# Row maxima of two neighbouring heads, scored in two row strips of the array

## The chip, the cores and the metric

The kernel runs on one core of one Trainium2 chip. The metric is device time in microseconds (us) of one execution. The engines are named as in the profile: PE is TensorE's matmuls, PEld its weight loads, DVE is VectorE, ACT is ScalarE, POOL is GpSimd, SP is SyncE, which only issues DMAs here.

## The reference

A decoder of four layers runs over `x` of 8 batches x 256 positions x 128 channels. Each layer adds three residual blocks: self-attention, cross-attention to a context of 512 positions, and a feed-forward block. Four of the attention blocks share one code path and are what the change touches. They have 16 heads of 8 channels:

```python
# layers 0 and 2, cross-attention (layer 0 with a mask), 512 keys; layer 3, self- and cross-attention, causal, 256 keys
scores = einsum('bqhd,bkhd->bhqk', qh, kh) / sqrt(8)      # (8, 16, 256, 512) or (8, 16, 256, 256)
attn = softmax(scores, axis=-1)                           # masked first, where there is a mask
ctx = einsum('bhqk,bkhd->bqhd', attn, vh).reshape(8, 256, 128)
x = x + ctx @ Wo.T + bo                                   # layer 3's second also gates the context
```

## The kernel before

**Heads in the partitions.** A head has only 8 channels. Queries and keys are split into a rounded part and a remainder, and four products of parts stand for one product of full precision, so a head takes 8 x 4 = 32 rows. `mh_k` holds two neighbouring heads for each of 8 pairs: the even head in rows 0 to 31, the odd one in rows 32 to 63, zeros in rows 64 to 95. `mh_q` holds each head by itself in its own 32 of the first 64 rows; all other rows are zero, so a matmul over 96 rows (`TOP`) gives one head's scores. Rows 96 and 97 of `mh_q` take the negated row maximum, in two parts, with ones against it in `mh_k`.

**Two passes over the scores.** Pass one (`maxima`, line 510) makes the scores with queries in the partitions, so that VectorE can reduce along a row: `mh_sps` in PSUM, reduced into `mh_nm`. With 512 keys there are two matmuls of 96 rows x 512 columns a head, one for each half of the queries, each in a bank of its own, and each reduced by VectorE: `lowest` (line 520) where there is a mask, `tensor_reduce` (line 542) where there is none. In the causal stages one bank holds both halves, 128 and 256 columns wide. `turn` (line 544, GpSimd) splits the maxima of four heads, `turned` (line 554) transposes them on TensorE (`mh_mps`) and sends them by a DMA into `mh_q`. Pass two (`exps`, line 565) makes the scores again with keys in the partitions, `mh_bsps`, with the maximum subtracted by the two extra rows, and ScalarE takes the exponent into `mh_e`. `combine` (line 614) multiplies with the values for four heads at once, each into its own 32 columns of the array (`mh_ops`, 128*32). `divide`, `finish`, `project_out` and `normed` end a batch element.

**Order.** One loop over t = 16 b + h runs over the 128 heads of 8 batch elements. Step t does `maxima(t)`, after every fourth head `turn`; then a stretch of another layer's work, the guest (layer 0's own attention, `la_` tiles, in the first stage; other blocks, `fa_` and `qf_` tiles among them, in layer 2's and the first causal stage); then `turned` for the group before, at t % 4 == 1; `exps(t - lag)`, with a lag of 8 steps or of 12 in the causal stages; `combine` every fourth step; then what was put off. Matmuls and transposes keep the order in which they are written (`mm`, line 459, records them all, so they all have line 460; transposes have line 463).

**PSUM.** Eight banks: `ps_a` has three, used in turn by `mh_sps` and `mh_ops`; `ps_b` three for `mh_bsps`; `g` two for all else.

Of the kernel before, what the change touches and what calls it, by code (L numbers as in the profile page):

```python
# [30 lines left out]
F32 = mybir.dt.float32  # L31
BF16 = mybir.dt.bfloat16
# [4 lines left out]
ALU = mybir.AluOpType  # L37
AX = mybir.AxisListType
PSUM = bass.MemoryType.PSUM

P = 128
B, S, SK, D = 8, 256, 512, 128
# [4 lines left out]
TOP = 96  # L47
FLOOR = -1.0e20
# [296 lines left out]
class _Heads:  # L345
# [113 lines left out]
    def mm(self, *a, **kw):  # L459
        return self.E.tc.keep_in_program_order(self.E.nc.tensor.matmul(*a, **kw))  # L460
# [17 lines left out]
def _heads_attention(E, ctx, causal=False, mask=None, key_bias=None, gate=False, guest=None, known=(0,), pace=None):  # L478
# [6 lines left out]
    hd, nc, W = E.heads, E.nc, E.w(E.heads.layer)  # L485
    n, ready = hd.n, hd.ready
# [5 lines left out]
    wk = pool("mh", 2)  # L492
# [3 lines left out]
    ps_a = ctx.enter_context(E.tc.tile_pool(name="mh_pa", bufs=3, space=PSUM))  # L496
    ps_b = ctx.enter_context(E.tc.tile_pool(name="mh_pb", bufs=3, space=PSUM))
    mm = hd.mm
# [8 lines left out]

    units, extras = {}, {}

    def maxima(t):  # L510

        b, h = divmod(t, H)
        if h == 0 and key_bias:
            extras[b] = key_bias(b)
        if h % 4 == 0:
            u = units[t // 4] = SimpleNamespace(r=ready[b], es={}, extra=extras.get(b))
            u.nm = sm.tile([P, 2, 4], F32, name="mh_nm")
        u = units[t // 4]
        q, k = u.r.q[:TOP, h, :], u.r.k[:TOP, h // 2, :]
        def lowest(at, scores, lowered):  # L520

            rest = wk.tile([P, S if causal else n], BF16, name="mh_rest")
            nc.vector.tensor_tensor_reduce(  # L523
                rest[:, : scores.shape[1]], scores, lowered, -1.0, -FLOOR, ALU.add, ALU.min, accum_out=at
            )

        col = slice(h % 4, h % 4 + 1)
        if causal:
            ps = ps_a.tile([P, 3 * P], F32, tag="a", name="mh_sps")
            mm(ps[:, :P], q[:, :P], k[:, :P], start=True, stop=True, skip_group_check=True)  # L530
            mm(ps[:, P:], q[:, P:], k, start=True, stop=True, skip_group_check=True)
            by = (u.extra or E.causal)[0].rearrange("p i k -> p (i k)")
            lowest(u.nm[:, 0, col], ps[:, :P], by[:, :P])
            lowest(u.nm[:, 1, col], ps[:, P:], by[:, P:])
            return
        for c in range(2):
            ps = ps_a.tile([P, n], F32, tag="a", name="mh_sps")
            mm(ps, q[:, c * P : c * P + P], k, start=True, stop=True, skip_group_check=True)
            if mask is not None:
                lowest(u.nm[:, c, col], ps, mask[0][:, c, :])  # L540
            else:
                nc.vector.tensor_reduce(u.nm[:, c, col], ps, AX.X, ALU.max, negate=True)  # L542

    def turn(i):

        u = units[i]
        nm = u.nm
        hi = sm.tile([P, 2, 4], F32R, name="mh_hi")
        nc.gpsimd.tensor_copy(hi, nm)  # L549
        u.nx = sm.tile([P, 2, 2, 4], F32, name="mh_nx")  # L550
        nc.gpsimd.tensor_copy(u.nx[:, :, 0, :], hi)
        nc.gpsimd.tensor_tensor(u.nx[:, :, 1, :], nm, hi, ALU.subtract)  # L552

    def turned(i):

        u = units[i]
        ps = pg.tile([P, 2, P], F32, tag="g", name="mh_mps")
        for c in range(2):
            turn_over(ps[:8, c, :], u.nx[:, c, :, :].rearrange("p a h -> p (a h)"))
        m = wk.tile([8, S], F32R, name="mh_m")  # L560
        nc.scalar.copy(m, ps[:8].rearrange("p c q -> p (c q)"))  # L561
        h0 = 4 * (i % 4)
        nc.scalar.dma_start(u.r.q[TOP : TOP + 2, h0 : h0 + 4, :].bitcast(F32), m.bitcast(F32))

    def exps(t):

        u, h = units[t // 4], t % H
        if causal:
            ps = ps_b.tile([P, 384], F32, tag="b", name="mh_bsps")
            if u.extra:  # L570
                mm(ps, E.ident16, u.extra[1], start=True, stop=False, skip_group_check=True)
            else:
                mm(
                    ps.rearrange("p (i q) -> p i q", q=P)[:, 0:3:2, :], E.later,
                    E.ident16.unsqueeze(1).to_broadcast([P, 2, P]), start=True, stop=False, skip_group_check=True,
                )
            for kt in range(2):
                mm(
                    ps[:, 256 * kt : 256 + P * kt], u.r.k[:, h // 2, kt * P : kt * P + P],
                    u.r.q[:, h, kt * P :], start=False, stop=kt == 1, skip_group_check=True,  # L580
                )
            e = pe.tile([P, 384], F32, tag="e", name="mh_e")
            nc.scalar.activation(e, ps, AF.Exp, scale=scale)  # L583
            u.es[h % 4, 0], u.es[h % 4, 1] = e[:, :S], e[:, S:]
            return
        for kt in range(0, nk, 2):
            ps = ps_b.tile([P, 2, S], F32, tag="b", name="mh_bsps")
            if mask is not None:
                mm(ps, E.ident16, mask[1][:, kt : kt + 2, :], start=True, stop=False, skip_group_check=True)
            for j in range(2):  # L590
                mm(
                    ps[:, j, :], u.r.k[:, h // 2, (kt + j) * P : (kt + j + 1) * P], u.r.q[:, h, :],
                    start=mask is None, stop=True, skip_group_check=True,
                )
            e = pe.tile([P, 2, S], F32, tag="e", name="mh_e")
            nc.scalar.activation(e, ps, AF.Exp, scale=scale)  # L596
            u.es[h % 4, kt], u.es[h % 4, kt + 1] = e[:, 0, :], e[:, 1, :]
# [5 lines left out]
    def gate_of(b):  # L603
        ps = pg.tile([P, 2, D], F32, tag="g", name="mh_gps")
        for c in range(2):
            mm(ps[:, c, :], E.xt(b)[:, c * P : c * P + P], W("wg"), start=True, stop=True)
        gates[b] = gp.tile([P, 2, D], F32, name="mh_gates")
        nc.vector.tensor_tensor(gates[b], ps, W("bg").unsqueeze(1).to_broadcast([P, 2, D]), ALU.add)

        nc.scalar.activation(gates[b], gates[b], AF.Exp, scale=-1.0)  # L610
        nc.vector.tensor_scalar(gates[b], gates[b], 1.0, None, ALU.add)
        nc.vector.reciprocal(gates[b], gates[b])  # L612
# [68 lines left out]
    def visit(rate):  # L681

        credit[0] += rate
        while credit[0] >= 1:
            credit[0] -= 1
            normed_already.add(next(guest, None))
# [3 lines left out]
    t, end = 0, H * B + lag + 4  # L690
    while t < end or todo:
        now[0] = t
        b, h = divmod(t, H)
        if b + 1 < B:
            if h == 0:
                early, spread, values = hd.steps(b + 1)
            if causal:

                at = {2: early[:1], 3: early[1:2], 4: early[2:], 13: [values]}
                at.update({5 + i: spread[i : i + 1] for i in range(6)})  # L700
            else:
                at = {6: early[:1], 8: spread[:1], 9: spread[1:2] + early[1:], 13: spread[5:] + [values]}
                at.update({10 + i: spread[2 + i : 3 + i] for i in range(3)})
            while h == (2 if causal else 9) and b + 1 not in normed_already:
                visit(1)
            for f in at.get(h, ()):
                f()
        if gate and b < B and h == 6:
            gate_of(b)
        if t < H * B:  # L710
            maxima(t)
            if t % 4 == 3:
                turn(t // 4)
        if guest:
            visit(pace(t))
        if t % 4 == 1 and 4 < t < H * B + 2:
            turned(t // 4 - 1)
        if 0 <= t - lag < H * B:
            exps(t - lag)
        c = t - lag - 4  # L720
        if c % 4 == 0 and 0 <= c < H * B:
            combine(c // 4)
        for f in todo.pop(t, ()):
            f()
        if t == H * (B - 2) + 12 + free:
            E.draining()
        if t in E.amid:
            E.amid.pop(t)()
        t += 1
# [4 lines left out]
def _l0(E, names, given_up):  # L734

    nc = E.nc
    with ExitStack() as scope, ExitStack() as first:
# [39 lines left out]
        for _ in queries:  # L777
            pass
        _heads_attention(E, scope, mask=(m, mt), guest=steps, pace=lambda t: 2.4 if t < 9 else 1.4)


def _l2_xattn(E, ctx):
    guest, E.guest = E.guest, None
    _heads_attention(E, ctx, guest=guest, known=(0, 1), pace=lambda t: 1.25)


def _l3_attn(E, ctx):
    guest, E.guest = E.guest, None
    _heads_attention(E, ctx, causal=True, guest=guest, known=(0, 1), pace=lambda t: 0.6)
# [992 lines left out]
```

## Time and profile before

| | |
|---|---|
| median of two runs | 1774.6 us (1774.25 and 1774.94) |
| span of the profiled execution, first to last instruction | 1770.2 us |
| PE busy | 1462.7 us, 83% |
| PEld busy | 1055.3 us, 60% |
| DVE busy | 1148.5 us, 65% |
| ACT busy | 881.5 us, 50% |
| POOL busy | 495.7 us, 28% |
| mean granted TensorE clock | 0.928 |
| `mh_sps` matmuls, 96x512 | 512, mean 457 ns |
| `mh_sps` matmuls, 96x256 and 96x128 | 256 each, mean 355 and 322 ns |
| reduction of 128x512 scores on DVE | 685 ns with the mask, 680 without |

The profile is of one execution. A matmul's row lasts from its start to its modelled end, and rows overlap, so what a matmul costs TensorE is read from one start to the next. "128x512" is partitions x elements; "96*128" are the rows and columns of the array that an instruction uses. "[0.19 <-PE mh_sps L460]" at a row's end says that the engine stood idle for 0.19 us before it and what it waited for. A line of waits gives the total in us, the number of times, and the longest. A line of a window gives its start and end, its length, then for each engine busy time and the number of instructions, and then the granted clock, the share of the DMA engines and GB/s.

The four stages of the change lie at 62 to 495 us (layer 0), 894 to 1265 (layer 2), 1339 to 1510 and 1528 to 1690 (layer 3).

### The profile page before, as it was taken

Reading aid. Unit: us, or ns where it says so; the run is one execution under the profiler, and the core shown is the slowest. Engines: PE = TensorE matmul, PEld = TensorE weight load, DVE = VectorE, ACT = ScalarE, POOL = GpSimd, SP = SyncE. Lnnn points to the kernel's source line nnn. Section 1 sums busy time; section 2 is a strip of 40 time slices with the busy share of each in tenths; the row PEclk is TensorE's granted clock in tenths of the full one; section 3 lists DMA queues with packets and bytes.
Section 4 is the critical chain, followed back from the end, with each engine's and each line's share of the span. In section 5 each row is a group of like instructions: output and inputs, shape, how many; then the busy total and the mean of one; then the engine's idle time right before and its main releaser. Section 6 shows DMA issues by size and latency. Waiting matters only on the chain. (4 is left out here: it accounts for less than half of the span.)

```text
span 1770.2 us, 29308 instructions
## 1 busy us (share of the span) xinstructions
PE 1462.7 (83%) x10103; PEld 1055.3 (60%) x10141; DVE 1148.5 (65%) x3857; ACT 881.5 (50%) x1830; POOL 495.7 (28%) x987
## 2 busy tenths in 40 slices
PE   5689989999999998785578888878946799799986
PEld 3457677766665555453446666656615677677763
DVE  4567666765636676777667777767465666466756
ACT  7245455555652344325535655557644466355543
POOL 3122222221110122223433433332113433244422
PEclk9799999999999999997979999989956899899998
DMA  4011011104100000000111101111002221122100
GB/s 154 13 37 36 6 34 37 36 11 155 38 1 1 1 1 1 0 1 1 36 35 36 28 14 37 37 37 45 2 10 65 85 69 38 50 55 59 39 1 25
DMA packets 47236, 60.43 MB, mean 34 GB/s; under 512 B 5232, under 2 KB 36976, under 8 KB 46448
## 3 DMA queue, kind: packets, MB, share of 16 engines
q1 hardware_dynamic: 44720, 56.99, 11.9%
q8 instruction: 80, 1.31, 0.3%
q10 hardware_dynamic: 2368, 1.57, 0.3%
q14 instruction: 68, 0.56, 0.1%
HBM read 14.50 MB, written 1.05 MB: 9 GB/s over the span
## 5 line engine op out<-in xcount | busy, mean ns | idle before, releaser
L460 PE MATMUL mh_sps<-mh_k,mh_q 96*128 96x512 f32 (+2 forms) x1024 | 323.4, 398 | 49.0 <-DMA mh_q<-mh_qp 16.9
L460 PE MATMUL mh_bsps<-mh_q,mh_k 128*128 128x256 f32 (+1 forms) x1536 | 352.7, 335 | 7.6 <-ACT mh_e L596 4.1
L596 ACT ACTIVATE mh_e<-mh_bsps 128x512 f32<-128x512 f32 x512 | 281.0, 599 | 117.6 <-PE mh_bsps L460 110.4
L460 PEld LDWEIGHTS mh_bsps<-mh_q,mh_k 128*128 128x128 f32 x1536 | 265.8, 198 | 32.6 <-issue 6.9
L460 PEld LDWEIGHTS mh_sps<-mh_k,mh_q 96*128 96x128 f32 x1024 | 172.5, 202 | 96.2 <-issue 35.9
L523 DVE CUSTOM_DVE_ANT_0 mh_rest<-mh_sps,mask_b 128x512 bf16<-128x512 f32 x256 | 167.2, 685 | 81.4 <-PE mh_sps L460 78.4
L460 PE MATMUL mh_ops<-mh_e,mh_v 128*32 128x256 f32 (+1 forms) x3072 | 194.0, 373 | 1.3 <-DVE mh_nm L523 0.8
L542 DVE TENSOR_REDUCE mh_nm<-mh_sps 128x1 f32<-128x512 f32 x256 | 165.0, 680 | 25.7 <-PE mh_sps L460 25.2
L583 ACT ACTIVATE mh_e<-mh_bsps 128x384 f32<-128x384 f32 x256 | 118.6, 494 | 57.8 <-PE mh_bsps L460 33.5
L460 PEld LDWEIGHTS mh_ops<-mh_e,mh_v 128*32 128x32 f32 x3072 | 94.5, 111 | 66.1 <-ACT mh_e L583 5.8
L197 POOL TENSOR_SCALAR ln_rstd<-ln_mv 128x2 f32<-128x2 f32 x96 | 22.0, 229 | 386.4 <-DVE ln_mv L195 386.1
L549 POOL CAST mh_hi<-mh_nm 128x8 fp32r<-128x8 f32 x128 | 25.0, 195 | 337.9 <-DVE mh_nm L523 211.4
L523 DVE CUSTOM_DVE_ANT_0 mh_rest<-mh_sps,causal 128x128 bf16<-128x128 f32 (+1 forms) x256 | 79.4, 352 | 51.0 <-PE mh_sps L460 49.0
L523 DVE CUSTOM_DVE_ANT_0 mh_rest<-mh_sps,km_q 128x128 bf16<-128x128 f32 (+1 forms) x256 | 79.4, 350 | 43.8 <-PE mh_sps L460 42.5
L561 ACT CAST mh_m<-mh_mps 8x256 fp32r<-8x256 f32 x128 | 46.2, 361 | 102.1 <-PE mh_mps L463 100.2
L215 ACT COPY xt<-ln_ps 128x256 f32<-128x256 f32 x96 | 36.0, 375 | 120.5 <-PE ln_ps L463 62.3
L629 ACT COPY mh_osb<-mh_ops 128x256 f32<-128x256 f32 x128 | 47.7, 372 | 83.5 <-PE mh_ops L460 83.3
L886 ACT ACTIVATE moe_si<-moe_gps 128x512 f32<-128x512 f32 x64 | 38.0, 597 | 102.5 <-PE moe_gps L884 87.6
L460 PE MATMUL mh_bsps<-mask_t,ident 128*128 128x512 bf16 x219 | 84.7, 387 | 0.4 <-ACT mh_e L596 0.4
L201 DVE TENSOR_SCALAR ln_z<-x,ln_mv,ln_rstd 128x128 f32<-128x128 f32 x136 | 43.4, 360 | 54.9 <-POOL ln_rstd L198 54.7
L884 PE MATMUL moe_ups<-xt,w_L_ffn 128*128 128x512 f32 x128 | 69.2, 623 | 6.9 <-ACT moe_si L886 4.8
L463 PE MATMUL mh_mps<-ident,mh_nx 128*8 128x128 f32 x256 | 51.1, 282 | 27.7 <-POOL mh_nx L552 23.2
(360 smaller groups left out, 3086.8 us busy)
## 6 DMA issues: line engine op xcount, KB each, us to landing
mh_k<-mh_kp SPq DMA_DIRECT2D x64, 256.0 KB
mh_q<-mh_qp SPq DMA_DIRECT2D x256, 64.0 KB
mh_k<-mh_kp SPq DMA_DIRECT2D x64, 128.0 KB
w_L_ffn<-in_w_L_ffn SPq DMA_DIRECT2D x2, 1558.0 KB
w_L_attn<-in_w_L_attn SPq DMA_DIRECT2D x2, 1056.0 KB
ctx_t<-in_ctx_t SPq DMA_DIRECT2D x4, 512.0 KB
mh_q<-mh_m ACTq DMA_DIRECT2D x128, 8.0 KB
w_L_ffn<-in_w_L_ffn SPq DMA_DIRECT2D x2, 687.0 KB
```

Of the source, the lines that this page charges most:

```text
L201: (engine or nc.vector).tensor_scalar(z[:, q, :], E.x[:, 2 * b + q, :], mv[:, q, 0:1], rstd[:, q : q + 1], ALU.subtract, ALU.mult)
L215: E.nc.scalar.copy(E.xt(b), ps.rearrange("p q t -> p (q t)"))
L460: return self.E.tc.keep_in_program_order(self.E.nc.tensor.matmul(*a, **kw))
L463: return self.E.tc.keep_in_program_order(self.E.nc.tensor.transpose(*a))
L523: nc.vector.tensor_tensor_reduce(rest[:, : scores.shape[1]], scores, lowered, -1.0, -FLOOR, ALU.add, ALU.min, accum_out=at)
L542: nc.vector.tensor_reduce(u.nm[:, c, col], ps, AX.X, ALU.max, negate=True)
L561: nc.scalar.copy(m, ps[:8].rearrange("p c q -> p (c q)"))
L583: nc.scalar.activation(e, ps, AF.Exp, scale=scale)
L596: nc.scalar.activation(e, ps, AF.Exp, scale=scale)
L629: nc.scalar.copy(osbs[b][:, u4 % 2, :], ops)
L884: nc.tensor.matmul(ps, W("w13")[:, o : o + P], xt, start=True, stop=True)
L886: nc.scalar.activation(si, pgate, AF.Silu)
```

## The change

`maxima` is called at even steps only and does two heads, t and t + 1. Each head's matmul takes only the head's own 32 rows, 0 to 31 or 32 to 63, of `mh_q` and `mh_k`, so that the two heads stand in two row strips of the array. The two heads' matmuls of one query half stand next to each other in the order and write two banks of `ps_a`. With 512 keys the two first halves are made and their reductions issued, then the two second halves; in the causal stages all four matmuls come first and then the four reductions. `lowest` moves out of `maxima` as it is. `turn` and all else stay where they were.

```diff
--- before.py
+++ after.py
@@ -507,6 +507,13 @@
 
     units, extras = {}, {}
 
+    def lowest(at, scores, lowered):
+
+        rest = wk.tile([P, S if causal else n], BF16, name="mh_rest")
+        nc.vector.tensor_tensor_reduce(
+            rest[:, : scores.shape[1]], scores, lowered, -1.0, -FLOOR, ALU.add, ALU.min, accum_out=at
+        )
+
     def maxima(t):
 
         b, h = divmod(t, H)
@@ -516,30 +523,32 @@
             u = units[t // 4] = SimpleNamespace(r=ready[b], es={}, extra=extras.get(b))
             u.nm = sm.tile([P, 2, 4], F32, name="mh_nm")
         u = units[t // 4]
-        q, k = u.r.q[:TOP, h, :], u.r.k[:TOP, h // 2, :]
-        def lowest(at, scores, lowered):
-
-            rest = wk.tile([P, S if causal else n], BF16, name="mh_rest")
-            nc.vector.tensor_tensor_reduce(
-                rest[:, : scores.shape[1]], scores, lowered, -1.0, -FLOOR, ALU.add, ALU.min, accum_out=at
-            )
-
-        col = slice(h % 4, h % 4 + 1)
+        two = range(2)
+        rows = [slice(32 * r, 32 * r + 32) for r in two]
+        q = [u.r.q[rows[r], h + r, :] for r in two]
+        k = [u.r.k[rows[r], h // 2, :] for r in two]
+        col = [slice((h + r) % 4, (h + r) % 4 + 1) for r in two]
+        go = dict(start=True, stop=True, skip_group_check=True)
         if causal:
-            ps = ps_a.tile([P, 3 * P], F32, tag="a", name="mh_sps")
-            mm(ps[:, :P], q[:, :P], k[:, :P], start=True, stop=True, skip_group_check=True)
-            mm(ps[:, P:], q[:, P:], k, start=True, stop=True, skip_group_check=True)
+            ps = [ps_a.tile([P, 3 * P], F32, tag="a", name="mh_sps") for r in two]
+            for r in two:
+                mm(ps[r][:, :P], q[r][:, :P], k[r][:, :P], **go)
+            for r in two:
+                mm(ps[r][:, P:], q[r][:, P:], k[r], **go)
             by = (u.extra or E.causal)[0].rearrange("p i k -> p (i k)")
-            lowest(u.nm[:, 0, col], ps[:, :P], by[:, :P])
-            lowest(u.nm[:, 1, col], ps[:, P:], by[:, P:])
+            for r in two:
+                lowest(u.nm[:, 0, col[r]], ps[r][:, :P], by[:, :P])
+                lowest(u.nm[:, 1, col[r]], ps[r][:, P:], by[:, P:])
             return
         for c in range(2):
-            ps = ps_a.tile([P, n], F32, tag="a", name="mh_sps")
-            mm(ps, q[:, c * P : c * P + P], k, start=True, stop=True, skip_group_check=True)
-            if mask is not None:
-                lowest(u.nm[:, c, col], ps, mask[0][:, c, :])
-            else:
-                nc.vector.tensor_reduce(u.nm[:, c, col], ps, AX.X, ALU.max, negate=True)
+            ps = [ps_a.tile([P, n], F32, tag="a", name="mh_sps") for r in two]
+            for r in two:
+                mm(ps[r], q[r][:, c * P : c * P + P], k[r], **go)
+            for r in two:
+                if mask is not None:
+                    lowest(u.nm[:, c, col[r]], ps[r], mask[0][:, c, :])
+                else:
+                    nc.vector.tensor_reduce(u.nm[:, c, col[r]], ps[r], AX.X, ALU.max, negate=True)
 
     def turn(i):
 
@@ -708,7 +717,8 @@
         if gate and b < B and h == 6:
             gate_of(b)
         if t < H * B:
-            maxima(t)
+            if t % 2 == 0:
+                maxima(t)
             if t % 4 == 3:
                 turn(t // 4)
         if guest:
```

## The prediction

> **What bounds the kernel now.** I read the page first, then the busy time by stage, then the timeline instruction by instruction, then the waits. The page names TensorE; its chain that ended last covers only some 7% of the span and decides nothing.
>
> ```profile
> PE 1462.7 (83%) x10103; PEld 1055.3 (60%) x10141; DVE 1148.5 (65%) x3857; ACT 881.5 (50%) x1830; POOL 495.7 (28%) x987
> ```
>
> The changed code runs in four stages: layer 0's and layer 2's attention over 512 keys (two banks per head), and layer 3's two causal attentions (one bank per head). The windows of those four, with busy time of PE, PEld, DVE, ACT, POOL, then granted clock:
>
> ```profile
> 62.00:495.00 433.00, 398.09 (x2901) 296.82 (x2939) 288.25 (x827) 224.26 (x498) 98.99 (x195) 0.98 0.15 40
> 894.00:1265.00 371.00, 312.79 (x2273) 227.06 (x2272) 276.56 (x696) 208.98 (x452) 121.57 (x223) 0.94 0.13 32
> 1339.00:1510.00 171.00, 148.53 (x1342) 122.53 (x1345) 108.45 (x644) 93.53 (x225) 64.87 (x175) 0.91 0.22 63
> 1528.00:1690.00 162.00, 144.76 (x1317) 120.27 (x1320) 108.83 (x622) 88.36 (x218) 66.67 (x176) 0.97 0.18 49
> ```
>
> PE is busy 92%, 84%, 87% and 89% of these. Its matmuls keep program order, so whatever one of them waits for, all behind it wait for. Time put on PE is time on the path, except where it falls on PE's own idle time: 35, 58, 22 and 17 us.
>
> **What a score matmul costs today, with 512 keys.** The timeline of the second stage, a step with PE running freely:
>
> ```profile
> 1008.30 0.63 PE L460 MATMUL mh_sps<-mh_k,mh_q 96*128 96x512 f32 x2
> 1008.53 0.14 PEld L463 LDWEIGHTS fa_tps<-ident,fa_o 128*128 128x128 f32 x1
> 1008.73 0.69 DVE L542 TENSOR_REDUCE mh_nm<-mh_sps 128x1 f32<-128x512 f32 x1 [0.19 <-PE mh_sps L460]
> 1008.76 0.27 PE L463 MATMUL fa_tps<-ident,fa_o 128*128 128x128 f32 x1
> ```
>
> Two start at 1008.30 and the next work at 1008.76: 0.23 us a slot, though one lasts 0.39 from start to end. Their weight loads are hidden: one is done while the matmul before it streams. Two heads are four slots, 0.94 us. The reduction starts 0.04 us after its matmul's end and takes 0.68.
>
> Here a page disagrees. The Trainium skill (TensorE: Matmul & The Clock Gate, Part 3, what overlaps and what doesn't) says that a weight load overlaps a matmul in flight only when their row groups differ. The load at 1008.53 runs under a full-array score matmul and its own matmul follows in the normal slot, so the trace disagrees. By the rule four slots would cost about 0.11 us more each, 1.38 us, and the loss below would be near 0.54 us a pair in place of 0.98; I go by the trace.
>
> **What the change removes and adds on PE.** It halves the streaming: two heads' matmuls go in two 32-row strips and may run side by side. The trace has no row strips, but it has column strips, `mh_ops` (128*32), which show two things at once:
>
> ```profile
> 1001.06 0.40 PE L460 MATMUL mh_bsps<-mh_q,mh_k 128*128 128x256 f32 x2
> 1001.39 0.62 PE L460 MATMUL mh_ops<-mh_e,mh_v 128*32 128x256 f32 x5
> ...
> 1002.71 0.61 PE L460 MATMUL mh_ops<-mh_e,mh_v 128*32 128x256 f32 x8
> 1003.25 0.50 PE L460 MATMUL mh_sps<-mh_k,mh_q 96*128 96x512 f32 x1
> ...
> 1003.25 0.73 PE L460 MATMUL mh_sps<-mh_k,mh_q 96*128 96x512 f32 x2
> ...
> 1003.79 1.29 DVE L542 TENSOR_REDUCE mh_nm<-mh_sps 128x1 f32<-128x512 f32 x2 [1.00 <-PE mh_sps L460]
> ```
>
> Strips do run together: 32 `mh_ops` matmuls take 1.93 us, groups of four 0.22 apart. And entering or leaving them empties the array. The last `mh_bsps` starts at 1001.18, its 0.12 slot ends at 1001.30, and the strips begin at 1001.39: 0.10. On the way out the last group's slot ends near 1003.15, the next load starts at 1003.25: 0.10 again, and the first matmul then takes 0.50, not 0.39: its load of 0.11 has nothing to hide under. Today full-array scores pay none of this, unless they stand behind `mh_ops`. After, every pair pays 0.10 + 0.11 going in and 0.10 + 0.11 coming out. I take the column strips' prices for row strips; the bounds are none of it and twice it.
>
> **The buffer wait.** With 512 keys the pair needs four banks (two heads, two query halves) and `ps_a` has three. The fourth matmul, second head and second half, must go into the bank that the first filled, and so waits until VectorE has reduced that one. Today the bank is asked for one step later, and PE does the exponents' matmuls in between. What such a wait costs is in the trace:
>
> ```profile
> 958.50 1.28 DVE L542 TENSOR_REDUCE mh_nm<-mh_sps 128x1 f32<-128x512 f32 x2
> ...
> 959.24 0.19 PEld L460 LDWEIGHTS mh_sps<-mh_k,mh_q 96*128 96x128 f32 x1 [0.27 <-DVE mh_nm L542]
> ```
>
> The first of the two reductions ends at 959.18, the load starts at 959.24: 0.06 for the release, and the load is exposed. One pair then runs: empty array 0.10, first load and matmul 0.50, to VectorE 0.04, reduction 0.68, release 0.06, fourth matmul's load and slot 0.34 (1003.25 to the second start, 1003.98 - 0.40 = 1003.58, gives 0.33), empty array 0.10, exposed load of what follows 0.11. Sum 1.92 us, against 0.94 today: **0.98 us more a pair**. The second and third matmuls lie inside the wait, so whether strips overlap makes no difference here. Queued behind the waiting load on PE: the guest layer's matmuls, the maxima's transposes, `mh_bsps`, `mh_ops`; ScalarE's exponents wait for those. 64 pairs in each of two stages, 128 x 0.98 = **+125 us**.
>
> VectorE may be late when the first matmul ends. Pairing matmuls and reductions in the timeline, a step's first reduction starts 0.23 us after the matmul in layer 0 and 0.65 in layer 2 on the mean (median 0.04). That would add 64 x (0.19 + 0.61) = 51 us; but a slower PE lets VectorE catch up. Bounds 0 and 51, I take **+25**.
>
> Existing idle time of PE swallows part. In layer 0, 35 us less two waits of 11 us for DMAs leave 24; in layer 2 it is 58, among it 15 us in which scores wait for these very reductions. Bounds 0 and 82, I take half, **-41**.
>
> **The causal stages.** Two banks suffice for a pair, so no wait arises. Price today:
>
> ```profile
> 1600.46 0.44 PE L460 MATMUL mh_sps<-mh_k,mh_q 96*128 96x128 f32 x2
> 1600.74 0.34 PE L460 MATMUL mh_bsps<-km_k,ident 128*128 128x384 bf16 x1
> ```
>
> 0.28 us a head, 0.57 a pair. After: 0.10 + 0.11, then the wide matmuls' loads 0.11 (longer than the narrow streams they cover), the wide streams 0.11, 0.10 out, and up to 0.11 for an exposed load of the mask's weights (a bf16 load's row is half as long, so about 0.05): 0.58. Nothing gained or lost. If row strips ran one after the other, loads included, a pair would pay up to 0.30 more: 128 x 0.30 = 38 us. The Trainium skill (same page and part, the measured speedup) gives four row strips 3.07 times the throughput; no run here shows it, and by it the 38 us fall away.
>
> Something moves to the good. Both heads' maxima are now asked for at the even step, so the last of a group of four is ready a step before `turned` wants it. The waits of PE in the two causal windows are:
>
> ```profile
> PE mh_mps L463 <- POOL mh_nx L552: 13.4, 10, 4.2
> PE mh_mps L463 <- POOL mh_nx L552: 9.5, 14, 1.2
> ```
>
> Bounds 0 and -23, I take **-10**. `lowest` is only moved; the number and shape of VectorE's instructions, of `turn` and of all DMAs stay. SP's, POOL's and ScalarE's queues keep their order but for the earlier maxima.
>
> **Sum.** 125 + 25 - 41 - 10 = +99 us on the profiled span of 1770.2, so 1869. The runs' median of 1774.6 lies 4.4 above that span (launch and end): **1874 us**, 5.6% slower.
>
> **Rivals.** First, row strips don't overlap. For it: no row strip in the trace; against it: column strips do. The 512-key stages hardly change, the causal ones pay 38: 1912 us. Second, PE's idle swallows nearly all that it can: 125 - 82 - 23 = +20, 1795 us. For it: layer 2 has 58 us of idle and a VectorE busy 75%; against it: layer 0's PE is at 92%, and its waits are on guests' chains, not beside the scores. Third, on the other side: the fourth matmul's wait costs nothing, because VectorE, not PE, sets the pace and PE would have waited as long elsewhere. A pair then costs 0.42 of switching and 0.46 of streaming, 0.88 against 0.94, which is -8 us in all, and the causal waits vanish, -23: 1744 us. It decides only if PE's idle beside the scores were near 0.98 us a pair; the 15 us in layer 2 over 64 pairs are 0.23.
>
> **How the numbers follow.** Forecast 0.62, no overlap 0.18, mostly swallowed 0.12, costless 0.08. About 2% (35 us) is what a measurement of this kernel tells from no change. Under the forecast the slowdown is over 2% nearly always; the second rival lies within, the third within or beyond on the fast side. That gives faster 0.04, same 0.12, slower 0.84. The range runs from 1808 (most idle swallowed) to 1935 (no overlap, and VectorE late).
>
> **What would show it.** Right: in the 512-key stages a wait of PE or of its weight loads on VectorE's reductions of scores (`mh_nm`), 128 times and 0.7 us or more each; score matmuls 32*128 with two starts some 10 ns apart; those two stages longer by about 40 to 60 us each; the causal stages within some 10 us of today, with `mh_mps` waiting less. Wrong: the fourth score matmul starting with no wait, the two stages longer by under 20 us each, or starts in a causal pair 0.1 us apart or more.

## The result, and the profile after

The changed kernel takes 1926.95 us (median of two runs, 1923.32 and 1930.59) against 1774.6: ratio 1.0862, 95% interval 1.0811 to 1.0913, so 8.6% slower. Its profiled execution has a span of 1921.5 us, 151 more than before; I forecast 99 more.

The first block of its page shows the same work on every engine but TensorE's own:

```profile
PE 1549.5 (81%) x10141; PEld 1028.7 (54%) x10141; DVE 1150.3 (60%) x3857; ACT 879.8 (46%) x1830; POOL 493.0 (26%) x987
```

The windows of layer 0's stage, layer 2's stage, and the two causal stages together:

```profile
63.00:558.00 495.00, 430.28 (x2933) 291.15 (x2934) 287.77 (x829) 221.92 (x497) 99.86 (x196) 0.95 0.13 35
958.00:1425.00 467.00, 364.44 (x2275) 227.72 (x2274) 282.15 (x696) 209.90 (x451) 120.31 (x223) 0.84 0.11 26
1497.00:1841.00 344.00, 308.75 (x2759) 227.59 (x2760) 216.33 (x1277) 187.28 (x459) 133.66 (x359) 0.89 0.20 56
```

From the first to the last score matmul, layer 0's stage goes from 432 to 493 us (+61), layer 2's from 370 to 464 (+94), the causal stages from 350 to 343 (-7); the stretch between layers 0 and 2, which the change does not touch, grows by 3. The last column but two is the granted clock: 0.95, 0.84 and 0.89, where it was 0.98, 0.93 and 0.94 before. In the records the clock is either full or half, so a mean of 0.84 over 467 us says that some 150 us ran at half clock; before, it was 49.

One pair with 512 keys, in the timeline of layer 0's stage at full clock:

```profile
203.88 0.29 PEld L460 LDWEIGHTS mh_sps<-mh_k,mh_q 32*128 32x128 f32 x3
203.88 0.73 PE L460 MATMUL mh_sps<-mh_k,mh_q 32*128 32x512 f32 x3
...
204.41 0.69 DVE L513 CUSTOM_DVE_ANT_0 mh_rest<-mh_sps,mask_b 128x512 bf16<-128x512 f32 x1 [2.21 <-PE mh_sps L460]
...
205.16 0.18 PEld L460 LDWEIGHTS mh_sps<-mh_k,mh_q 32*128 32x128 f32 x1 [0.99 <-DVE mh_nm L513]
205.16 0.50 PE L460 MATMUL mh_sps<-mh_k,mh_q 32*128 32x512 f32 x1 [0.56 <-DVE mh_nm L513]
205.59 0.53 PEld L463 LDWEIGHTS la_tps<-ident,la_ek 128*128 128x128 f32 x5 [0.24 <-issue]
```

Three matmuls go without a wait (the first two start 3 ns apart, the third 0.33 us after them), VectorE reduces the first bank from 204.41 to 205.10, and only then does the fourth start, at 205.16. The next work begins at 205.59, 1.71 us after the pair's start. The waits of PE, in layer 0's, in layer 2's and (two lines) in the causal window:

```profile
PE mh_sps L460 <- DVE mh_nm L513: 41.7, 64, 1.9
...
PE mh_sps L460 <- DVE mh_nm L551: 68.1, 63, 7.3
...
PE mh_sps L460 <- DVE mh_nm L513: 13.3, 14, 3.1
PE mh_mps L463 <- POOL mh_nx L561: 12.1, 10, 2.8
```

The same waits on `mh_nm` before, in the same three:

```profile
PE mh_sps L460 <- DVE mh_nm L523: 1.4, 2, 0.8
...
PE mh_sps L460 <- DVE mh_nm L542: 15.0, 9, 4.6
...
PE mh_sps L460 <- DVE mh_nm L523: 5.7, 6, 2.1
```

In the 512-key stages every pair but one waits, where 2 and 9 times a score matmul waited before. The causal stages lost half of their wait for the maxima's transposes, 22.9 us before; their wait on `mh_nm` grew by 8 us.

At half clock the same steps look like this, in layer 2:

```profile
1045.31 1.22 PE L460 MATMUL mh_sps<-mh_k,mh_q 32*128 32x512 f32 x3
...
1046.88 0.79 PE L460 MATMUL mh_sps<-mh_k,mh_q 32*128 32x512 f32 x1 [0.36 <-DVE mh_nm L551]
```

A matmul with an exposed load lasts 0.79 us where it lasts 0.50 at full clock.

### The profile page after: what moved, and what is told of

The parts are those of the page before. It is cut to its first block, busy times and chain, and to the rows that moved or that the text cites. A ratio compares the mean times of both kernels' runs of the same rounds, so it can differ in the third digit from the quotient of the medians.

```text
span 1921.5 us, 29406 instructions
## 1 busy us (share of the span) xinstructions
PE 1549.5 (81%) x10141; PEld 1028.7 (54%) x10141; DVE 1150.3 (60%) x3857; ACT 879.8 (46%) x1830; POOL 493.0 (26%) x987
## 4 chain that ended last, share of the span: by engine, by line
PE 54%; DVE 22%; POOL 9%; issue 7%; ACT 6%; DMA 2%; SPq 1%; ACTq 0%; POOLq 0%; DVEq 0%
PE mh_bsps L460 10%; PE mh_ops L460 9%; PE mh_sps L460 7%; DVE mh_nm L551 3%; PE fa_kvps L460 3%; DVE mh_rest L513 2%; POOL ln_rstd L198 2%; PE moe_dps L905 2%; PE moe_gps L894 2%; PE moe_ups L894 2%; PE la_cps L460 2%; PE la_qps L460 2%; PE mh_mps L463 1%; DVE ln_z L201 1%; ACT mh_e L605 1%
## 5 line engine op out<-in xcount | busy, mean ns | idle before, releaser
L460 PE MATMUL mh_bsps<-mh_q,mh_k 128*128 128x256 f32 (+1 forms) x1536 | 364.1, 345 | 3.4 <-ACT mh_e L605 3.2
L460 PE MATMUL mh_sps<-mh_k,mh_q 32*128 32x512 f32 (+2 forms) x1024 | 242.9, 425 | 143.4 <-DVE mh_nm L551 68.1
L460 PEld LDWEIGHTS mh_bsps<-mh_q,mh_k 128*128 128x128 f32 x1536 | 273.1, 205 | 35.2 <-issue 12.7
L460 PEld LDWEIGHTS mh_sps<-mh_k,mh_q 32*128 32x128 f32 x1024 | 110.9, 197 | 255.8 <-DVE mh_nm L551 98.9
L460 PE MATMUL mh_ops<-mh_e,mh_v 128*32 128x256 f32 (+1 forms) x3072 | 212.0, 407 | 1.8 <-DVE mh_nm L551 1.6
L513 DVE CUSTOM_DVE_ANT_0 mh_rest<-mh_sps,mask_b 128x512 bf16<-128x512 f32 x256 | 162.9, 686 | 65.9 <-PE mh_sps L460 59.8
L460 PE MATMUL mh_bsps<-mask_t,ident 128*128 128x512 bf16 x256 | 100.3, 392 | 0.3 <-ACT mh_e L605 0.3
L905 PEld LDWEIGHTS moe_dps<-w_L_ffn,moe_act 128*128 128x128 f32 x512 | 66.1, 204 | 15.7 <-issue 8.0
L894 PE MATMUL moe_gps<-xt,w_L_ffn 128*128 128x512 f32 x128 | 70.5, 634 | 4.2 <-DVE moe_act L897 4.2
```

The lines of the kernel that those rows point to most:

```text
L513: nc.vector.tensor_tensor_reduce(rest[:, : scores.shape[1]], scores, lowered, -1.0, -FLOOR, ALU.add, ALU.min, accum_out=at)
L894: nc.tensor.matmul(ps, W("w13")[:, o : o + P], xt, start=True, stop=True)
L905: nc.tensor.matmul(ps[:, t, :], act[:, c, t * P : t * P + P], W("w2")[:, o : o + P], start=c == 0, stop=c == 1)
```

## Experiments

All stand beside runs of the kernel before, on the same chip (1773.4 to 1773.9 us). Three theories: W, the fourth matmul's wait for its bank makes most of the loss; S, emptying the array for the strips does; C, the granted clock falls, either because PE idles more or because strips keep fewer rows busy. Lengths in the table run from a stage's first score matmul to its last; the clock is that of the stage's window. A time in the table is one execution, but for the kernel before, the change, e_banks0 and e_banks (two each), e_causal and e_causal96 (six) and e_early (seven); stages and clocks are of one profiled execution each. Twelve runs of the kernel before, on one chip, had mean clocks of 0.921 to 0.930, which is 280 to 248 us at half clock in the whole kernel: two traces whose half-clock times differ by less than some 30 us are not told apart by that alone.

| kernel | time, us | layer 0, us | layer 2, us | causal, us | clock in the three |
|---|---|---|---|---|---|
| before | 1774.6 | 432 | 370 | 350 | 0.98, 0.93, 0.94 |
| the change | 1927.0 | 493 | 464 | 343 | 0.95, 0.84, 0.89 |
| e_order | 1862.7 | 471 | 427 | 339 | 0.97, 0.89, 0.91 |
| e_halves | 1804.7 | 446 | 397 | 339 | 0.97, 0.88, 0.90 |
| e_strip | 1954.8 | 470 | 416 | 444 | 0.95, 0.86, 0.76 |
| e_strip64 | 1892.4 | 466 | 416 | 391 | 0.96, 0.86, 0.90 |
| e_fill | 1913.8 | 486 | 460 | 341 | 0.97, 0.84, 0.91 |
| e_orderfill | 1861.7 | 470 | 432 | 339 | 0.99, 0.92, 0.91 |
| e_banks0 | 1785.3 | 432 | 369 | 353 | 0.98, 0.93, 0.92 |
| e_banks | 1823.8 | 443 | 409 | 342 | 0.97, 0.87, 0.91 |
| e_causal | 1767.5 | 434 | 373 | 342 | 0.97, 0.92, 0.90 |
| e_causal96 | 1761.4 | 432 | 370 | 338 | 0.98, 0.93, 0.91 |
| e_early | 1768.2 | 435 | 370 | 344 | 0.98, 0.93, 0.92 |

### The pairing without strips (e_order)

```diff
-        rows = [slice(32 * r, 32 * r + 32) for r in two]
+        rows = [slice(0, TOP) for r in two]
```

> The pairing alone: two heads made back to back in the same order and banks as in the changed kernel, but each over 96 rows, so no row strips and no emptying of the array. Theory W (the wait of the fourth matmul for its bank makes most of the loss): a pair with 512 keys takes 0.39 + 0.04 + 0.68 + 0.06 + 0.34 = 1.51 us against 0.94, +0.57 x 128 = 73 us, and with the changed kernel's excess over my sum (152 measured for 99) up to 100: 1835 to 1875 us, with some 128 waits of PE on mh_nm. Theory S (emptying the array for the strips makes most of it): within 20 us of 1775. Theory C (row strips lower the granted clock, since they keep fewer rows busy): the half-clock time of layer 2's stage goes back from 151 to about 50 us; if idle time lowers it, it stays above 100.

1862.7 us, inside W's range. The two 512-key stages are 39 and 57 us longer than before with no row strip anywhere, so 96 of the 155 us that they lose come from the order and its bank alone. Layer 2's window, and PE's wait in it:

```profile
935.00:1364.00 429.00, 328.58 (x2272) 227.30 (x2272) 280.67 (x695) 208.51 (x450) 120.46 (x222) 0.89 0.12 28
...
PE mh_sps L460 <- DVE mh_nm L551: 63.0, 61, 7.3
```

The wait is nearly the changed kernel's 68.1, but the clock is 0.89: 90 us at half clock, between the 49 of before and the 151 of the change. S is out as the main cause. Both readings of C keep a share: without strips part of the low clock goes, and part stays with the idle time.

### Strips without the wait (e_halves)

```diff
-    def maxima(t):
+    def maxima(t, half=None):
...
-        for c in range(2):
+        for c in (half,):
...
-            if t % 2 == 0:
+            if not causal:
+                maxima(t - t % 2, t % 2)
+            elif t % 2 == 0:
                 maxima(t)
```

> Row strips without the bank wait: with 512 keys the two heads' first halves are made at the even step, the second halves at the odd step, so that a bank is asked for again as late as before the change; the causal stages are as in the changed kernel. W: the waits on mh_nm go back to the level of before, a pair pays twice 0.42 of switching and 0.23 of streaming, 1.30 us against 0.94, +46 us, less some 10 swallowed and 8 from the causal stages: 1795 to 1825 us. S: 1900 us or more, since there are twice as many switches. C by strips: half-clock time in layer 2 stays near 150 us; C by idle time: it falls below 100.

1804.7 us, as W said: the stages are 14 and 27 us longer than before, with twice as many switches into strips as in the change. The wait is back at the level of before:

```profile
911.00:1309.00 398.00, 345.18 (x2273) 222.74 (x2273) 278.82 (x696) 209.94 (x451) 121.68 (x222) 0.88 0.12 30
...
PE mh_sps L460 <- DVE mh_nm L551: 11.7, 9, 2.9
```

The clock is the surprise. PE is idle for 53 us, no more than before (398 less 345; it was 58), and yet 99 us run at half clock against 49: neither near 150 nor clearly below 100, so neither reading of C alone. The clock is lower with no more idle time. But idle time is counted between matmuls' rows, which last longer than the streaming in them; the stage has 128 switches of some 0.42 us, by estimate 54 us in all, in which little or nothing streams, and no run separates that from the strips as such. The two shares nearly add up: 41 us more at half clock from the wait (e_order), 51 more from the strips (e_halves), 102 more from both.

### Strips without pairing, of 32 and of 64 rows (e_strip, e_strip64)

```diff
-        q, k = u.r.q[:TOP, h, :], u.r.k[:TOP, h // 2, :]
+        own = slice(32 * (h % 2), 32 * (h % 2) + 32)
+        q, k = u.r.q[own, h, :], u.r.k[own, h // 2, :]     # e_strip
+        q, k = u.r.q[:64, h, :], u.r.k[:64, h // 2, :]     # e_strip64, in its place
```

> The strips alone: the order of before, one head a step, each head over its own 32 rows. Nothing runs beside anything, and each step switches into the strips and back. At the column strips' prices (0.42 a switch in and out with exposed loads): 0.89 against 0.47 us a head with 512 keys, +0.42 x 256 = 108 us; causal 0.58 against 0.285, +0.30 x 256 = 77 us; some 40 swallowed by idle time: 1900 to 1960 us. If a switch costs row strips nothing: within 10 us of 1775. Waits on mh_nm as in the kernel before under every theory.

> As e_strip, one head a step and no pairing, but each head over 64 rows (its own 32 and the other head's, which hold zeros in the queries), so strips of 64 rows: the array is emptied as often, and twice as many rows take part. If the lower clock of e_strip (212 us at half clock in the two causal stages against 44 before, with less idle time of PE than before) comes from the emptying: 190 to 230 us, and 1940 to 1965 us in all. If it comes from the few rows that take part: 100 to 150 us at half clock, 1905 to 1930 us. If emptying happens for 32-row strips alone: within 15 us of 1774.

1954.8 us, inside its range, and 1892.4, below every range given for it. At full clock both pay the same, 0.66 us a head with 512 keys from the first start to the next other work (0.87 with the forecast's 0.10 and exposed load of 0.11 around it, for an expected 0.89), and 0.42 in the causal stages. A pair of strips in the changed kernel takes 0.43 there: two heads for the time of one, so strips do run together. In the causal windows the two kernels differ in one thing:

```profile
1427.00:1872.00 445.00, 420.10 (x2761) 294.10 (x2761) 227.29 (x1279) 195.58 (x460) 134.89 (x359) 0.76 0.16 43
...
1416.00:1809.00 393.00, 368.26 (x2768) 261.06 (x2771) 227.20 (x1284) 193.42 (x462) 135.20 (x360) 0.90 0.18 49
```

The first is 32 rows, the second 64. The same prices, the same 25 us of idle time, the same number of emptyings, but 212 against 81 us at half clock, and 53 us between the stages' lengths: 0.40 us lost for each us at half clock. Nearly all of that difference lies in the second of the two causal stages:

```profile
1639.00:1872.00 233.00, 224.38 (x1307) 157.31 (x1306) 112.46 (x617) 92.04 (x216) 65.97 (x175) 0.68 0.12 34
...
1625.00:1809.00 184.00, 175.52 (x1314) 125.67 (x1316) 112.66 (x622) 90.22 (x218) 66.36 (x176) 0.93 0.16 43
```

There 147 against 26 us run at half clock; in the first causal stage it is 64 against 54, and in the 512-key stages 42 and 120 with 32 rows, 32 and 116 with 64. So the number of rows in use is a likely cause of the fall in one stage (81 us in all, where I expected 100 to 150), on one execution of each kernel, and of none that can be told apart in the other three. What lowers the clock in layer 2, 116 to 120 us at half clock against 49 with less idle time than before, stays open: the switching and the use of fewer than 96 rows are not separated.

### Filling the wait (e_fill, e_orderfill)

```diff
             for r in two:
-                mm(ps[r], q[r][:, c * P : c * P + P], k[r], **go)
+                for _ in range(4 if c == 1 and r == 0 else 1):
+                    mm(ps[r], q[r][:, c * P : c * P + P], k[r], **go)
```

> The changed kernel, with the third score matmul of each 512-key pair (first head, second half) issued four times into the same bank with the same values, three of them idle work that fills the wait for the fourth bank with 0.69 us of streaming. C by idle time: the half-clock time in layer 2 falls from 151 us to under 100 and the whole gets faster by 15 to 50 us, 1875 to 1910. C by strips, or a clock that has nothing to do with PE's idle time: half-clock time stays at 130 or more, and the time stays at 1920 to 1940, since the added matmuls lie inside the wait.

> The pairing over 96 rows (e_order, 1862.7 us, 90 us at half clock in layer 2's stage), with the third score matmul of each 512-key pair issued four times into the same bank, as in e_fill but 96 rows wide. C by idle time: idle work over 96 rows keeps the clock up, half-clock time in layer 2 falls from 90 us to 60 or less, 1835 to 1855 us. If such filling does nothing for the clock, as with 32 rows in layer 2 (e_fill, 144 us against 151): 80 or more, 1858 to 1870 us.

e_fill: 1913.8 us, and layer 2 still has 144 us at half clock, though PE's idle time in that stage falls from 102 to 66 us. Only layer 0's falls, from 49 to 29 us, and its stage gets 7 us shorter. e_orderfill, over 96 rows: 72 us at half clock in layer 2 against e_order's 90, between the two expectations, and 1861.7 us, no faster. 1913.8 lies between the two ranges given for e_fill, 1861.7 inside the one for filling that does nothing. A fall by 7 us at half clock, or by 18, is within what runs of one kernel differ by, so a lift of the clock in layer 2 is not shown, and the filling buys almost nothing. It fills only some 0.7 us of a wait: in e_fill 12 waits on `mh_nm` of up to 5.3 us, 31.7 us in all, are left in layer 2, so the long waits are not tested by it. That idle time alone sets the clock is refuted by e_halves and e_strip, where the clock falls with no more of it; that it has a share is not.

### Four banks (e_banks, and its control e_banks0)

```diff
-    ps_a = ctx.enter_context(E.tc.tile_pool(name="mh_pa", bufs=3, space=PSUM))
-    ps_b = ctx.enter_context(E.tc.tile_pool(name="mh_pb", bufs=3, space=PSUM))
+    ps_a = ctx.enter_context(E.tc.tile_pool(name="mh_pa", bufs=4, space=PSUM))
+    ps_b = ctx.enter_context(E.tc.tile_pool(name="mh_pb", bufs=2, space=PSUM))
```

> Control for the next one: the kernel before with four banks for the row maxima's scores and two, not three, for the exponents' scores. ScalarE then holds the exponents' banks more often: between 0 and +60 us, 1775 to 1835. No theory of the change is at stake.

> The changed kernel with four banks for the row maxima's scores (and two for the exponents'), so that a pair with 512 keys never waits for its own first bank. W: a pair costs 0.88 us against 0.94, so the time is within 25 us of the control's, and the 128 waits on mh_nm of 0.7 us or more vanish. S or C by strips: 50 us or more slower than the control.

The control costs 11 us (ratio 1.0066, 1.0049 to 1.0084). With the change on top it is 1823.8, ratio to the kernel before 1.0283 (1.0266 to 1.0301): 103 us better than the change, 38 above the control, between the 25 that W allowed and the 50 that S, or C by strips, asked for. The pair itself is cured, 0.66 us from start to next work and 0.87 with its edges. But the wait has a new place in layer 2:

```profile
1102.80 2.48 DVE L551 TENSOR_REDUCE mh_nm<-mh_sps 128x1 f32<-128x512 f32 x4
1103.53 1.45 PEld L460 LDWEIGHTS mh_ops<-mh_e,mh_v 128*32 128x32 f32 x32 [1.16 <-DVE mh_nm L551]
...
PE mh_ops L460 <- DVE mh_nm L551: 27.0, 13, 6.0
```

`mh_ops` takes its banks from the same ring, and with four of them its turn falls on the pair's first bank. Four reductions stand in one block of 2.5 us on VectorE. The lower clock (106 us at half clock in layer 2) stays too.

### The causal stages alone (e_causal, e_causal96, e_early)

e_causal keeps the changed `maxima` for the causal stages and runs the 512-key stages as before; e_causal96 is the same over 96 rows; e_early is the kernel before with each causal head's maxima one step earlier:

```diff
-            maxima(t)
+            if not causal:
+                maxima(t)
+            else:
+                for ahead in ((0, 1) if t == 0 else (t + 1,)):
+                    if ahead < H * B:
+                        maxima(ahead)
```

> Strips and pairs in the two causal stages alone; the 512-key stages run exactly as before the change. Strips run together and the maxima come a step earlier: 5 to 15 us faster, 1760 to 1770 us, with PE waiting less for mh_nx. Rival: the gain seen in one trace is chance or is paid back by a lower granted clock: 1772 to 1780.

> As the one before, but the causal pairs over 96 rows, without strips: only the order of the matmuls is changed. If the gain of the causal stages comes from the maxima being ready a step earlier, it is the same, 1760 to 1770 us; if it comes from two strips running together, 1773 to 1780.

> Causal stages only: one head at a time over 96 rows as before, but each head's maxima one step earlier (head t + 1 at step t). If e_causal96's gain (ratio 0.9935) comes from the maxima being ready earlier for the transposes: the same or a little more, 1755 to 1766 us, with PE's wait for mh_nx down from 22.9 us to under 12. If it comes from two heads' matmuls standing together: 1771 to 1777 us.

Ratios to the kernel before: e_causal 0.9966 (0.9953 to 0.9979), e_causal96 0.9935 (0.9914 to 0.9956), e_early 0.9968 (0.9957 to 0.9980). All three gain under 1%, and no interval reaches 1. e_causal96 is the fastest here, 12 us under the kernel before, and it has no row strip in it. Being early makes half of that: e_early's median lies just past the end of its range, and PE's wait is down as expected:

```profile
PE mh_mps L463 <- POOL mh_nx L552: 9.8, 8, 3.2
```

The other half is the standing together, which I had not counted. Four full-array score matmuls in a row:

```profile
1603.89 0.68 PE L460 MATMUL mh_sps<-mh_k,mh_q 96*128 96x128 f32 x4
1604.41 0.34 PE L460 MATMUL mh_bsps<-km_k,ident 128*128 128x384 bf16 x1
```

take 0.52 us where two separate heads take 0.57; 128 pairs x 0.05 is 6 us, and the causal stages of e_causal96 are 6 us shorter than e_early's. The change's strips take less still:

```profile
1603.80 0.49 PE L460 MATMUL mh_sps<-mh_k,mh_q 32*128 32x128 f32 x4
1604.23 0.28 PE L460 MATMUL mh_bsps<-ident,causal 128*128 128x256 bf16 x1
```

0.43 us, but with 0.10 of emptying before it and an exposed load behind it. Over six runs each the mean clock is 0.917 with the strips (e_causal) and 0.922 without (e_causal96), and the strips come out 6 us behind by the medians; the two intervals just overlap.

## Why the prediction was right, and where it was short

**The pair's price was right.** 1.92 us a pair was forecast; of it 1.71 lies between the pair's start and the next work, and 1.71 was measured from 203.88 to 205.59; the median of all pairs at full clock is 1.72 and 1.70 in the two stages. (The other 0.21 are the forecast's 0.10 ahead and 0.11 for the load behind.) The column strips' prices held for row strips, and the strips overlap, so the first rival (no overlap) falls.

**VectorE's lateness was right.** PE's idle time on `mh_nm` grew by 40 us in layer 0 and by 53 in layer 2. A punctual wait shows as 0.56 in the row at 205.16, so 64 of them are 36; the rest, 4 and 17 us, is lateness, where I took 25 in all.

**The swallowed idle was too much in layer 2.** PE's idle time other than on `mh_nm` fell from 33 to 23 us in layer 0 (window less busy less wait: 495 - 430 - 42 after) and from 43 to 35 in layer 2 (467 - 364 - 68 after): 10 and 8 us, where I had 12 and 29. That half of it would be swallowed was a guess without a row behind it. This step is off by 23 us.

**The granted clock was not in the sum.** Every price was taken at full clock and the clock taken as given. It gave 161 us more at half clock over the four stages (30, 102 and 29). In layer 2, 63 + 17 - 8 = 72 us are explained by the other terms, and 94 were measured; the 22 left over against 102 us at half clock are 0.2 us for each, and e_strip against e_strip64 showed 0.40 where PE was hardly ever idle. The 22 are what is left over, not a measurement of their own; layer 0 leaves 4 in the same way (63 + 4 - 10 = 57, measured 61).

**The causal stages were right in size, in part for other reasons.** -10 forecast, -7 measured. The wait for the transposes fell by 11 us as said. A strip pair cost what was forecast, and matmuls standing together, not strips, would have gained some 6 more. That no such wait arises there was not so: PE's wait on `mh_nm` rose from 5.7 to 13.3 us.

Of 52 us missing, the idle time less the smaller lateness explains about 20, the causal stages and the stretch between layers 0 and 2 explain 3 each, and about 26 are the remainder that I put down to the clock. The second rival, most of the loss swallowed, and the third, a costless wait, fall: about an eighth of the added time was swallowed (18 us of some 147).

**The range held in part by luck.** 1927 lies 8 us under its upper end of 1935, and layer 2 grew by 94 us where I had named 40 to 60 as the sign of being right. The upper end stood for strips that do not overlap and a late VectorE (whose terms give 1938, not 1935). Strips do overlap; what filled that room was the clock and the idle time that was not swallowed.

## What to carry to other kernels

Before two units are made back to back, count the buffers that one unit needs at once: a ring that was deep enough for every step in turn becomes a wait inside the pair, and adding a buffer can move that wait to the next user of the ring. Strips of the array pay where enough streaming is saved in them: going in and out cost 0.42 us here, nearly the 0.48 by which a pair's streaming with 512 keys shrinks (0.94 to 0.46 at the forecast's prices). And a sum of prices from a trace holds at that trace's clock: in these traces work with waits or with row strips was granted less.

## What the runs showed of the hardware

- Two row strips of 32 run fully together, weight loads too: their starts are mostly 3 ns apart, and two heads take 0.43 us in strips where one takes 0.42.
- Strips of 32 and of 64 rows cost the same at full clock: 0.66 us a head with 512 keys, 0.42 in the causal stages.
- With strips the granted clock was lower with no more idle time of PE: in layer 2 from 49 to 99 us at half clock (e_halves) and to 120 (e_strip). With 64 rows in place of 32 it was 81 us in place of 212 in the causal stages, nearly all of it in one of the two, on one execution each.
- Filling some 0.7 us of each wait of PE with idle matmuls did not pay: layer 2 had 144 us at half clock after 151 over 32 rows, and 72 after 90 over 96, differences that single traces do not tell apart.
